# Attention of a two-block network: groups of heads in pairs, maxima ten steps ahead, weighing in halves of the queries

## The chip, the cores and the metric

The kernel runs on one core of a Trainium2 chip. The metric is the device time of one execution in microseconds; lower is better. The engines that matter here are TensorE (PE in the profile, with its weight loads as PEld), VectorE (DVE), ScalarE (ACT) and GpSimd (POOL). Each takes its own instructions strictly in order, and they wait for each other by semaphores.

## The reference

The network has two blocks over x of shape (8, 512, 128): attention with 16 heads and a mixture of experts, then a state-space layer and a second mixture of experts. Only the first attention is touched by the change:

```python
h = _layernorm(x, axis=-1) * (1 + ca) + sa
Q, K, V = (_lora_linear(h, W, b, A, B).reshape(8, 512, 16, 8) for q, k, v)
energy = jnp.einsum('nqhd,nkhd->nhqk', Q, K) / jnp.sqrt(8)
attn = jax.nn.softmax(energy, axis=-1)
out = jnp.einsum('nhqk,nkhd->nqhd', attn, V).reshape(8, 512, 128)
x = x + ga * _lora_linear(out, Wo, bo, Ao, Bo)
```

All of it is float32. The softmax subtracts each query's largest score, so the maxima have to be known before the exponentials.

## The kernel before

**Groups.** A head has 8 channels, so a 32-channel quarter of the 128 partitions holds four heads. A group g (32 of them: 8 batches by m = 0..3) is one head from each quarter, head 4j + m for j = 0..3. `split` (L465) writes the group's masked copies of queries and keys (`qt`, `kt`, 128x512) on POOL. The keys' copy carries a 1 in one otherwise unused row per quarter.

**Maxima.** For a unit u (a group's 128 queries, of which there are 4 x 32 = 128) `maxima` (L475) multiplies queries by keys into a pair of PSUM banks `pm` and DVE reduces each to its largest value, two heads at a time, into a padded tile `mpad`. When the four units of a group are through, `max_done` (L514) transposes `mpad` on PE (`pmt`, four transposes) and DVE subtracts the result from `qt`; the row of the queries' copy that meets the keys' 1 then holds minus the largest score.

**Scores, exponentials, weighing.** For a step t (a group's 128 keys) `scores` (L522) multiplies keys by queries into `ps`, one bank per head, and ACT takes the exponential into SBUF (`es`). `weigh` (L544) multiplies the values, 32 columns per head with a column of ones, by the exponentials: one call for 128 queries, 16 matmuls, into one bank `av`, which ACT copies to `part`. `normalise` (L564) transposes `part` back on PE (`ppt`), and DVE divides by the sums of the ones' column.

**Order.** The order is written out by hand. A step has two slots, so the 128 steps are slots 0 to 255; `slot` (L893) issues two score matmuls, two maxima matmuls of unit t + LEAD (LEAD = 6), two exponentials, one reduction, and then whatever `at_slot` has put into that slot. Units 0 to 5 come before slot 0, one in each second slot, through `maxima_first` (L495) with four matmuls and three reductions each, and small matmuls on the identity (`keep_busy`) between them. The last six steps have no maxima left. In the slots counted from a group's first one, a group's `split` is at -16, `max_done` at -3, `weigh` at 9, 11, 12 and 13, `normalise` at 15. A batch takes 32 slots, and what it needs besides (statistics of rows `load_stats` and `out_stats` on DVE, `load_batch`, `project_batch` with `pqk`, `values` with `pv`, `channels_back` with `pot` and `wo`, `out_proj` with `py`, and the routing of the tokens to experts) has slots of its own from L616 on; the slots of the routing are at L883 to L892.

**PSUM.** Of the eight banks four form the ring `sc` (`bank`, L307), which scores, `av`, `pmt`, `ppt` and all small results take in turn, each waiting until the tile four places before it has been read. The other four are two pairs `mx` (`pair`, L304) for the maxima and for `pqk`. All engine instructions but those of PE are issued by a helper, so the profile gives them line L65.

Of the kernel before, what the change touches and what calls it, by code (L numbers as in the profile page):

```python
# [10 lines left out]
FP = mybir.dt.float32  # L11
# [3 lines left out]
ALU = mybir.AluOpType  # L15
# [3 lines left out]
B, S, D = 8, 512, 128  # L19
P = 128  # L20
NC4 = S // P
NT = B * NC4
NE, NF = 8, 4
HD = 8
# [44 lines left out]
def tile_adaln_two_blocks(  # L69
# [41 lines left out]
    ident = ct([P, P], "ident")  # L111
# [62 lines left out]
    zeros = ct([P, P], "zeros")  # L174
    V.memset(zeros, 0.0)
    mpads = []
    for m in range(4):
        mp = ct([P, NC4, P], f"mpad{m}")
        G.memset(mp, 0.0)
        mpads.append(mp)  # L180
# [102 lines left out]

    mv1, rs1 = new_stats("l0a")
    mv2, rs2 = new_stats("l0f")
    LEAD = 6
    STEPS = 4 * 4 * B
    ES = 28
    kp = ctx.enter_context(tc.tile_pool(name="kp", bufs=1, side="right"))
# [2 lines left out]
    with tc.tile_pool(name="at", bufs=2) as at, tc.tile_pool(name="sc", bufs=4, space=PSUM) as psc, tc.tile_pool(  # L292
# [5 lines left out]
        for i in range(2):  # L298
            va = ate.tile([P, NC4, 16, 32], FP, tag=f"vaug{i}", name=f"vaug{i}")
            G.memset(va, 0.0)  # L300
            G.memset(va[:, :, :, HD], 1.0)
            vaugs.append(va)

        def pair(name):  # L304
# [146 lines left out]
        def values(b):  # L451
            ht = batch[b]["ht"]
            ps = bank("pv")
            for c in range(NC4):
                pin(
                    T.matmul(
                        ps[:, c, :], lhsT=ht[:, c * P : (c + 1) * P], rhs=wqk[:, 2, :], start=True, stop=True
                    )
                )
            A.copy(  # L460
                vaugs[b % 2].rearrange("p c h r -> p (c h) r")[:, :, 0:HD],
                flat(ps).rearrange("p (c d) -> p c d", d=HD),
            )

        def split(g):  # L465

            b, m = g // 4, g % 4
            sp = (m + 1) % 4
            qt = ate.tile([P, S], FP, tag="qt", name="qt", bufs=3)
            kt = ate.tile([P, S], FP, tag="kt", name="kt", bufs=3)  # L470
            (V if g == 0 else G).tensor_scalar(qt, batch[b]["q"], mask[:, m : m + 1], zero, ALU.mult, ALU.add)
            G.tensor_scalar(kt, batch[b]["k"], mask[:, m : m + 1], spare[:, sp : sp + 1], ALU.mult, ALU.add)
            group[g] = (qt, kt)

        def maxima(u, half):  # L475

            g, qc = u // 4, u % 4
            qt, kt = group[g]
            r0 = HD * ((g + 1) % 4)
            pm = pair("pm")  # L480
            for i in range(2):
                r = 32 * (2 * half + i)
                pin(
                    T.matmul(  # L484
                        pm[:, i, :],
                        lhsT=qt[r : r + 32, qc * P : (qc + 1) * P],
                        rhs=kt[r : r + 32, :],
                        start=True,
                        stop=True,
                    )  # L490
                )
            mp = mpads[g % 4][:, qc, :].rearrange("p (j r) -> p j r", r=32)
            return lambda: V.tensor_reduce(mp[:, 2 * half : 2 * half + 2, r0], pm, AX.X, ALU.max)

        def maxima_first(u):  # L495

            g, qc = u // 4, u % 4
            qt, kt = group[g]
            r0 = HD * ((g + 1) % 4)
# [9 lines left out]
            mp = mpads[g % 4][:, qc, :].rearrange("p (j r) -> p j r", r=32)  # L509
            V.tensor_reduce(mp[:, 0:2, r0], pm, AX.X, ALU.max)  # L510
            for j in (2, 3):
                V.tensor_reduce(mp[:, j : j + 1, r0], banks[j], AX.X, ALU.max)

        def max_done(g):  # L514

            qt, _ = group[g]
            pt = bank("pmt")
            for c in range(NC4):
                pin(T.transpose(pt[:, c, :], mpads[g % 4][:, c, :], ident))  # L519
            V.scalar_tensor_tensor(qt, flat(pt), -1.0, qt, ALU.mult, ALU.add)  # L520

        def scores(t, half):  # L522
            g, kc = t // 4, t % 4
# [17 lines left out]
                A.activation(es, ps, AF.Exp)  # L541
                es_of[t, j] = es

        def weigh(g, qc):  # L544

            b, m = g // 4, g % 4
            q = slice(P * qc, P * qc + P)
            ps = bank("av")
            for kc in range(NC4):
                for j in range(4):  # L550
                    pin(
                        T.matmul(  # L552
                            ps[32 * j : 32 * j + 32, 0, :],
                            lhsT=vaugs[b % 2][:, kc, 4 * j + m, :],
                            rhs=es_of[4 * g + kc, j][:, q],
                            start=(kc == 0),
                            stop=(kc == NC4 - 1),
                        )
                    )
            if qc == 0:  # L560
                part_of[g] = at.tile([P, NC4, P], FP, tag="part", name="part")
            A.copy(part_of[g][:, qc, :], ps[:, 0, :])

        def normalise(g):  # L564

            b, m = g // 4, g % 4
            part = part_of.pop(g)
            pt = bank("ppt")
            for c in range(NC4):
                pin(T.transpose(pt[:, c, :], part[:, c, :], ident))  # L570
            if m == 0:
                batch[b]["o"] = at.tile([P, NC4, D], FP, tag="o", name="o", bufs=1)
            p4 = pt.rearrange("p c (j r) -> p c j r", r=32)
            rd = stat.tile([P, NC4, 4], FP, tag="rd", name="rd")
            V.reciprocal(rd, p4[:, :, :, HD])
            o4 = batch[b]["o"].rearrange("p c (j m d) -> p c j m d", j=4, m=4)[:, :, :, m, :]
            V.tensor_tensor(o4, p4[:, :, :, 0:HD], rd.unsqueeze(3).to_broadcast([P, NC4, 4, HD]), ALU.mult)

        def channels_back(b):
            o = batch[b]["o"]  # L580
# [35 lines left out]
        at_slot(-42, silu_c)  # L616
        for t, n in ((-41, 9), (-31, 5), (-22, 3), (-16, 8), *((t, 5) for t in range(-11, 0, 2))):
            at_slot(t, lambda n=n: keep_busy(n))
        at_slot(-34, low_rank)
        at_slot(-33, lambda: modulation(0, mod0))  # L620
        at_slot(1, lambda: clamp(mod0, MOE_SCALE))
        at_slot(2, out_bias)
        at_slot(-9, lambda: modulation(1, mod1))
        at_slot(6, lambda: clamp(mod1, None))
        rows = ((gab, gab_rows), (mod0[:, 2, :], ga_rows), (mod0[:, 3, :], sb_rows), (mod0[:, 4, :], cb_rows))
        for i, (src, dst) in enumerate(rows):
# [1 line left out]
            at_slot(8 + i, lambda dst=dst, i=i: mod_rows_in(dst, i))  # L628
        for b in range(B):
            for c in range(NC4):  # L630
                at_slot(32 * b - 40 + c, lambda b=b, c=c: load_stats(b, c))
            if b == 0:
                at_slot(-35, lambda: load_root(0, 0))
                at_slot(-32, lambda: load_root(0, 1))
            else:
                at_slot(32 * b - 35, lambda b=b: load_root(b))
# [1159 lines left out]
```

## Time and profile before

| What | us |
|---|---|
| median of 3 runs | 1048.54 |
| lowest and highest run | 1046.57, 1048.92 |
| the profiled execution | 1048.89 |
| its span, first to last instruction | 1046.8 |
| first maxima matmul (L505) starts | 18.5 |
| first score matmul (L531) starts | 37.4 |
| last `av` matmul (L552) starts | 544.8 |

Attention therefore fills the stretch from 18.5 to about 546 us; the first mixture of experts follows, and its routing already runs on POOL and DVE within attention. The page gives each engine's busy time, the span in 40 slices, and the groups of like instructions. "idle before" is the time for which an engine stood still ahead of a group, and the arrow names what ended it.

### The profile page before, as it was taken

The numbers are of one execution on the slowest core, as the hardware profiler recorded it, in microseconds if no ns is written. First come the engines' busy times: TensorE is split into PE (matmuls) and PEld (weight loads), VectorE is DVE, ScalarE is ACT, GpSimd is POOL, SyncE is SP. The second block draws the span as 40 slices with busy tenths as digits, with TensorE's granted clock in tenths as the row PEclk, the third lists the DMA queues.
The fourth block names the chain that finished last, engine by engine and source line by source line (L and its number), as shares of the span: only waits on it lengthen the run. The fifth ranks groups of instructions, "written<-read, shape, count | busy, mean of one in ns | idle before, by whom it ended". The sixth has DMA issues, their size and how long they took to land.

```text
span 1046.8 us, 24415 instructions
## 1 busy us (share of the span) xinstructions
PE 1003.1 (96%) x9650; PEld 662.2 (63%) x9650; DVE 658.5 (63%) x1275; ACT 638.0 (61%) x1403; POOL 486.3 (46%) x764
## 2 busy tenths in 40 slices
PE   9999999999999999999999999999989978978888
PEld 7555555555555555555568989988778656655456
DVE  5968687777877777777712114136785649758572
ACT  1366667676766666666564655645686473685544
POOL 3313143463744547354364314278651457765651
PEclk9999999999999999999999999999999989999999
DMA  6099400000000000000126887722652043222051
GB/s 173 7 304 284 134 3 12 5 29 2 27 7 9 25 2 29 5 12 22 33 76 168 241 251 234 228 70 72 177 153 71 14 136 116 86 80 104 21 182 41
DMA packets 94771, 95.38 MB, mean 91 GB/s; under 512 B 7665, under 2 KB 72561, under 8 KB 94657
## 3 DMA queue, kind: packets, MB, share of 16 engines
q1 hardware_dynamic: 90384, 85.13, 26.7%
q0 software_dynamic: 4096, 8.40, 2.7%
q8 instruction: 76, 1.25, 0.5%
q14 instruction: 39, 0.31, 0.1%
q10 hardware_dynamic: 176, 0.30, 0.1%
HBM read 62.43 MB, written 31.36 MB: 90 GB/s over the span
## 4 chain that ended last, share of the span: by engine, by line
PE 76%; DVE 10%; POOL 5%; ACT 4%; issue 2%; DMA 2%; SPq 0%; ACTq 0%; POOLq 0%; DVEq 0%
PE ps L531 22%; PE av L552 11%; PE pyb L1044 9%; PE ph L1033 8%; PE pm L484 3%; DVE xc L65 2%; PE r L1440 2%; PE pe L1452 2%; PE pmt L519 2%; PE ppt L570 2%; PE pqk L444 1%; PE idle L417 1%; DVE sh L65 1%; PE pw L1352 1%; ACT L65 1%
## 5 line engine op out<-in xcount | busy, mean ns | idle before, releaser
L65 DVE TENSOR_REDUCE mpad<-pm 128x2 f32<-128x1024 f32 (+1 forms) x262 | 310.4, 1194 | 109.9 <-PE pm L484 106.8
L65 ACT ACTIVATE es<-ps 128x512 f32<-128x512 f32 x512 | 275.5, 598 | 161.3 <-PE pm L484 136.7
L531 PE MATMUL ps<-qt,kt 32*128 32x512 f32 x1024 | 291.2, 630 | 0.7 <-DVE x L65 0.6
L484 PE MATMUL pm<-kt,qt 32*128 32x512 f32 x976 | 261.5, 636 | 0.0
L552 PEld LDWEIGHTS av<-es,vaug 128*32 128x32 f32 x4096 | 104.2, 109 | 94.1 <-ACT part L65 43.2
L552 PE MATMUL av<-es,vaug 128*32 128x128 f32 x4096 | 137.7, 276 | 0.0
L531 PEld LDWEIGHTS ps<-qt,kt 32*128 32x128 f32 x1024 | 93.8, 183 | 61.2 <-issue 30.4
L65 ACT ACTIVATE hid<-ph,bias 128x256 f32<-128x256 f32 x184 | 72.0, 475 | 53.6 <-PE ph L1033 53.4
L786 POOL DMA_INDIRECT x_rows<-tok,ux x64 | 65.1, 1018 | 66.5 <-DMA x_rows<-tok,ux 58.4
L1044 PEld LDWEIGHTS pyb<-w2b,hid 128*128 128x128 f32 x736 | 89.7, 192 | 7.9 <-ACT hid L65 5.1
L1044 PE MATMUL pyb<-w2b,hid 128*128 128x128 f32 x736 | 91.2, 277 | 3.5 <-ACT hid L65 3.5
L1033 PE MATMUL ph<-xt,w1b 128*128 128x256 f32 x368 | 88.1, 383 | 0.0
L1064 POOL DMA_INDIRECT yg<-y_rows,yrows x64 | 66.8, 1043 | 35.9 <-issue 17.8
L484 PEld LDWEIGHTS pm<-kt,qt 32*128 32x128 f32 x976 | 73.2, 183 | 9.1 <-ACT kf L65 5.4
L65 POOL TENSOR_SCALAR qt<-qf,mask,zero 128x512 f32<-128x512 f32 x31 | 23.8, 768 | 110.1 <-PE pm L484 93.6
L1452 PE MATMUL pe<-x,l1w_sb 128*128 128x512 f32 x128 | 69.0, 635 | 4.6 <-ACT ye L65 4.5
L1033 PEld LDWEIGHTS ph<-xt,w1b 128*128 128x128 f32 x368 | 67.2, 193 | 7.5
L65 DVE COPY xt<-pxt 128x256 f32<-128x256 f32 x46 | 19.2, 419 | 76.2 <-PE pxt L958 76.2
L1440 PEld LDWEIGHTS r<-l1w_sb,t 128*128 128x128 f32 x368 | 47.9, 197 | 28.8 <-POOL t L65 13.7
L65 ACT ACTIVATE ye<-pe,pc 128x512 f32<-128x512 f32 x64 | 42.8, 682 | 37.3 <-PE pe L1452 28.3
L1440 PE MATMUL r<-l1w_sb,t 128*128 128x128 f32 x368 | 50.7, 283 | 10.8 <-POOL t L65 8.3
L65 DVE TENSOR_TENSOR t<-ye,gb 128x512 f32<-128x512 f32 x48 | 41.8, 892 | 1.8 <-DMA gb<-g_rows 0.9
(298 smaller groups left out, 1558.8 us busy)
## 6 DMA issues: line engine op xcount, KB each, us to landing
x_rows<-zeros SPq DMA_DIRECT2D x16, 1024.0 KB
gb<-g_rows SPq DMA_DIRECT2D x32, 512.0 KB
w1b<-in_w1t SPq DMA_DIRECT2D x46, 256.0 KB
w2b<-in_w2t SPq DMA_DIRECT2D x46, 256.0 KB
xg<-x_rows SPq DMA_DIRECT2D x46, 128.0 KB
y_rows<-yb SPq DMA_DIRECT2D x46, 128.0 KB
x<-in_x SPq DMA_DIRECT2D x8, 256.0 KB
h_chan<-hf SPq DMA_DIRECT2D x8, 256.0 KB
```

The lines of the kernel that those rows point to most:

```text
L65: return lambda *args, **kwargs: self.pin(call(*args, **kwargs))
L484: T.matmul(pm[:, i, :], lhsT=qt[r : r + 32, qc * P : (qc + 1) * P], rhs=kt[r : r + 32, :], start=True, stop=True,)
L519: pin(T.transpose(pt[:, c, :], mpads[g % 4][:, c, :], ident))
L531: T.matmul(ps, lhsT=kt[r : r + 32, kc * P : (kc + 1) * P], rhs=qt[r : r + 32, :], start=True, stop=True)
L552: T.matmul(ps[32 * j : 32 * j + 32, 0, :], lhsT=vaugs[b % 2][:, kc, 4 * j + m, :], rhs=es_of[4 * g + kc, j][:, q], start=(kc == 0), stop=( ...
L570: pin(T.transpose(pt[:, c, :], part[:, c, :], ident))
L786: nc.gpsimd.indirect_dma_start(out=x_rows[h], out_offset=IndirectOffsetOnAxis(ap=chosen["ux", b][:, k, c : c + 1], axis=0), in_=half[h]["t ...
L1033: pin(T.matmul(ph[:, f, :], lhsT=it["w1"][:, f * P : (f + 1) * P], rhs=it["x"], start=True, stop=True))
L1044: T.matmul(py[:, c, :], lhsT=it["hid"][:, f, c * P : (c + 1) * P], rhs=it["w2"][:, f, :], start=(f == 0 and "shared" not in it), stop=(f = ...
L1064: nc.gpsimd.indirect_dma_start(out=gathered[b][:, k, c, :], out_offset=None, in_=y_rows[h], in_offset=IndirectOffsetOnAxis(ap=half[h]["yro ...
L1440: T.matmul(ffn[b]["r"][:, c, :], lhsT=x[:, c * P : (c + 1) * P], rhs=w, start=(start and c == 0), stop=stop, skip_group_check=True,)
L1452: pin(T.matmul(pe, lhsT=l1w_sb[:, 2 + e, :], rhs=x1s[b], start=True, stop=True))
```

## The change

Two groups of one batch, g even and g + 1, become a pair.

- **Maxima in pairs.** The maxima of both groups go into one `mpad` tile, each in its own unused row of a quarter, so `max_done` runs once for a pair (slot -3 of its even group): four transposes, then two subtractions on DVE, one for each `qt`. Two `mpad` tiles are left of four.
- **LEAD is 10 instead of 6,** since both groups' maxima must be through before the even group's scores start. `split` moves from slot -16 to -24, and `qt` and `kt` get four buffers instead of three. Ten units come before slot 0.
- **Values.** The 32 columns of a head hold the 8 values and the column of ones at 0 to 8 for even m and at 16 to 24 for odd m. ACT's copy of a batch's values becomes two copies of half the size.
- **Weighing in halves.** One call handles 256 queries: 16 matmuls of 256 columns, in slots 9 and 12. The even group's result is copied to `part` by ACT; the odd group's is added to `part` by DVE.
- **Normalising in pairs.** One `normalise` per pair, at slot 23 of the even group: four transposes, one reciprocal and one product of twice the size.
- **Everything that feeds a batch** (`load_stats`, `load_root`, `load_batch` but for its middle step, `project_batch`) moves 8 slots ahead, `values` from slot 2 to slot -4 of its batch; the preparation before slot 0 moves 8 slots ahead too. The routing stays in its slots.

```diff
-    LEAD = 6
+    LEAD = 10
@@
-            A.copy(
-                vaugs[b % 2].rearrange("p c h r -> p (c h) r")[:, :, 0:HD],
-                flat(ps).rearrange("p (c d) -> p c d", d=HD),
-            )
+            for e in range(2):
+                A.copy(
+                    vaugs[b % 2].rearrange("p c (n e) r -> p (c n) e r", e=2)[:, :, e, 16 * e : 16 * e + HD],
+                    flat(ps).rearrange("p (n e d) -> p n e d", e=2, d=HD)[:, :, e, :],
+                )
@@
         def max_done(g):
-            qt, _ = group[g]
             pt = bank("pmt")
             for c in range(NC4):
-                pin(T.transpose(pt[:, c, :], mpads[g % 4][:, c, :], ident))
-            V.scalar_tensor_tensor(qt, flat(pt), -1.0, qt, ALU.mult, ALU.add)
+                pin(T.transpose(pt[:, c, :], mpads[g // 2 % 2][:, c, :], ident))
+            for k in range(2):
+                qt, _ = group[g + k]
+                V.scalar_tensor_tensor(qt, flat(pt), -1.0, qt, ALU.mult, ALU.add)
@@
-        def weigh(g, qc):
+        def weigh(g, h):
...
-            q = slice(P * qc, P * qc + P)
-            ps = bank("av")
+            q = slice(2 * P * h, 2 * P * h + 2 * P)
+            ps = flat(bank("av"))[:, 0 : 2 * P]
...
-            if qc == 0:
+            if g % 2:
+                part = flat(part_of[g - 1])[:, q]
+                V.tensor_tensor(part, part, ps, ALU.add)
+                return
+            if h == 0:
                 part_of[g] = at.tile([P, NC4, P], FP, tag="part", name="part")
-            A.copy(part_of[g][:, qc, :], ps[:, 0, :])
+            A.copy(flat(part_of[g])[:, q], ps)
@@
         for g in range(4 * B):
-            at_slot(8 * g - 16, lambda g=g: split(g))
-            at_slot(8 * g - 3, lambda g=g: max_done(g))
-            for qc in range(NC4):
-                at_slot(8 * g + (9, 11, 12, 13)[qc], lambda g=g, qc=qc: weigh(g, qc))
-            at_slot(8 * g + 15, lambda g=g: normalise(g))
+            at_slot(8 * g - 24, lambda g=g: split(g))
+            if g % 2 == 0:
+                at_slot(8 * g - 3, lambda g=g: max_done(g))
+                at_slot(8 * g + 23, lambda g=g: normalise(g))
+            for h in range(2):
+                at_slot(8 * g + (9, 12)[h], lambda g=g, h=h: weigh(g, h))
@@
-                at_slot(32 * b - 40 + c, lambda b=b, c=c: load_stats(b, c))
+                at_slot(32 * b - 48 + c, lambda b=b, c=c: load_stats(b, c))
...
-            for i, s in enumerate((-30, 20, -24)):
+            for i, s in enumerate((-38, 20, -32)):
...
-                at_slot(32 * b - 18 + i, lambda b=b, i=i: project_batch(b, i))
-            at_slot(32 * b + 2, lambda b=b: values(b))
+                at_slot(32 * b - 26 + i, lambda b=b, i=i: project_batch(b, i))
+            at_slot(32 * b - 4, lambda b=b: values(b))
```

More of the change, by code (lines that the diff above doesn't have):

```diff
@@ L176, in tile_adaln_two_blocks @@
     mpads = []
-    for m in range(4):
+    for m in range(2):
         mp = ct([P, NC4, P], f"mpad{m}")
@@ L300, in tile_adaln_two_blocks @@
             G.memset(va, 0.0)
-            G.memset(va[:, :, :, HD], 1.0)
+            for e in range(2):
+                G.memset(va.rearrange("p c (n e) r -> p c n e r", e=2)[:, :, :, e, 16 * e + HD], 1.0)
             vaugs.append(va)
@@ L459, in values @@
                 )
-            A.copy(
-                vaugs[b % 2].rearrange("p c h r -> p (c h) r")[:, :, 0:HD],
-                flat(ps).rearrange("p (c d) -> p c d", d=HD),
-            )
+            for e in range(2):
+                A.copy(
+                    vaugs[b % 2].rearrange("p c (n e) r -> p (c n) e r", e=2)[:, :, e, 16 * e : 16 * e + HD],
+                    flat(ps).rearrange("p (n e d) -> p n e d", e=2, d=HD)[:, :, e, :],
+                )
         def split(g):
             b, m = g // 4, g % 4
-            sp = (m + 1) % 4
-            qt = ate.tile([P, S], FP, tag="qt", name="qt", bufs=3)
-            kt = ate.tile([P, S], FP, tag="kt", name="kt", bufs=3)
+            sp = (m + 2) % 4
+            qt = ate.tile([P, S], FP, tag="qt", name="qt", bufs=4)
+            kt = ate.tile([P, S], FP, tag="kt", name="kt", bufs=4)
             (V if g == 0 else G).tensor_scalar(qt, batch[b]["q"], mask[:, m : m + 1], zero, ALU.mult, ALU.add)
@@ L478, in maxima @@
             qt, kt = group[g]
-            r0 = HD * ((g + 1) % 4)
+            r0 = HD * ((g + 2) % 4)
             pm = pair("pm")
@@ L491, in maxima @@
                 )
-            mp = mpads[g % 4][:, qc, :].rearrange("p (j r) -> p j r", r=32)
+            mp = mpads[g // 2 % 2][:, qc, :].rearrange("p (j r) -> p j r", r=32)
             return lambda: V.tensor_reduce(mp[:, 2 * half : 2 * half + 2, r0], pm, AX.X, ALU.max)
@@ L498, in maxima_first @@
             qt, kt = group[g]
-            r0 = HD * ((g + 1) % 4)
+            r0 = HD * ((g + 2) % 4)
             pm = pair("pm")
@@ L508, in maxima_first @@
                 )
-            mp = mpads[g % 4][:, qc, :].rearrange("p (j r) -> p j r", r=32)
+            mp = mpads[g // 2 % 2][:, qc, :].rearrange("p (j r) -> p j r", r=32)
             V.tensor_reduce(mp[:, 0:2, r0], pm, AX.X, ALU.max)
@@ L552, in weigh @@
                         T.matmul(
-                            ps[32 * j : 32 * j + 32, 0, :],
+                            ps[32 * j : 32 * j + 32, :],
                             lhsT=vaugs[b % 2][:, kc, 4 * j + m, :],
@@ L572, in normalise @@
                 batch[b]["o"] = at.tile([P, NC4, D], FP, tag="o", name="o", bufs=1)
-            p4 = pt.rearrange("p c (j r) -> p c j r", r=32)
-            rd = stat.tile([P, NC4, 4], FP, tag="rd", name="rd")
+            p4 = pt.rearrange("p c (j e r) -> p (c j) e r", j=4, e=2)
+            rd = stat.tile([P, NC4 * 4, 2], FP, tag="rd", name="rd")
             V.reciprocal(rd, p4[:, :, :, HD])
-            o4 = batch[b]["o"].rearrange("p c (j m d) -> p c j m d", j=4, m=4)[:, :, :, m, :]
-            V.tensor_tensor(o4, p4[:, :, :, 0:HD], rd.unsqueeze(3).to_broadcast([P, NC4, 4, HD]), ALU.mult)
+            o4 = batch[b]["o"].rearrange("p c (j m d) -> p (c j) m d", j=4, m=4)[:, :, m : m + 2, :]
+            V.tensor_tensor(o4, p4[:, :, :, 0:HD], rd.unsqueeze(3).to_broadcast([P, NC4 * 4, 2, HD]), ALU.mult)
         def channels_back(b):
@@ L609, in tile_adaln_two_blocks @@
         for g in range(4 * B):
-            at_slot(8 * g - 16, lambda g=g: split(g))
-            at_slot(8 * g - 3, lambda g=g: max_done(g))
-            for qc in range(NC4):
-                at_slot(8 * g + (9, 11, 12, 13)[qc], lambda g=g, qc=qc: weigh(g, qc))
-            at_slot(8 * g + 15, lambda g=g: normalise(g))
-        at_slot(-42, silu_c)
-        for t, n in ((-41, 9), (-31, 5), (-22, 3), (-16, 8), *((t, 5) for t in range(-11, 0, 2))):
+            at_slot(8 * g - 24, lambda g=g: split(g))
[4 more added lines that the diff above has]
+                at_slot(8 * g + (9, 12)[h], lambda g=g, h=h: weigh(g, h))
+        at_slot(-50, silu_c)
+        for t, n in ((-49, 9), (-39, 5), (-30, 3), (-24, 8), *((t, 5) for t in range(-19, 0, 2))):
             at_slot(t, lambda n=n: keep_busy(n))
-        at_slot(-34, low_rank)
-        at_slot(-33, lambda: modulation(0, mod0))
+        at_slot(-42, low_rank)
+        at_slot(-41, lambda: modulation(0, mod0))
         at_slot(1, lambda: clamp(mod0, MOE_SCALE))
         at_slot(2, out_bias)
-        at_slot(-9, lambda: modulation(1, mod1))
+        at_slot(-13, lambda: modulation(1, mod1))
         at_slot(6, lambda: clamp(mod1, None))
@@ L630, in tile_adaln_two_blocks @@
             for c in range(NC4):
-                at_slot(32 * b - 40 + c, lambda b=b, c=c: load_stats(b, c))
+                at_slot(32 * b - 48 + c, lambda b=b, c=c: load_stats(b, c))
             if b == 0:
-                at_slot(-35, lambda: load_root(0, 0))
-                at_slot(-32, lambda: load_root(0, 1))
-            else:
-                at_slot(32 * b - 35, lambda b=b: load_root(b))
-            for i, s in enumerate((-30, 20, -24)):
+                at_slot(-43, lambda: load_root(0, 0))
+                at_slot(-40, lambda: load_root(0, 1))
+            else:
+                at_slot(32 * b - 43, lambda b=b: load_root(b))
+            for i, s in enumerate((-38, 20, -32)):
                 at_slot(32 * b + s, lambda b=b, i=i: load_batch(b, i))
             for i in range(2):
-                at_slot(32 * b - 18 + i, lambda b=b, i=i: project_batch(b, i))
-            at_slot(32 * b + 2, lambda b=b: values(b))
+                at_slot(32 * b - 26 + i, lambda b=b, i=i: project_batch(b, i))
+            at_slot(32 * b - 4, lambda b=b: values(b))
             at_slot(32 * b + 42, lambda b=b: channels_back(b))
```

## The prediction

> **What bounds the kernel now.** I read the page's busy shares first, then the groups by shape, then the timeline of one stretch of eight slots, and last the waits at attention's end.
>
> ```profile
> PE 1003.1 (96%) x9650; PEld 662.2 (63%) x9650; DVE 658.5 (63%) x1275; ACT 638.0 (61%) x1403; POOL 486.3 (46%) x764
> ...
> L65 DVE TENSOR_REDUCE mpad<-pm 128x2 f32<-128x1024 f32 (+1 forms) x262 | 310.4, 1194 | 109.9 <-PE pm L484 106.8
> L65 ACT ACTIVATE es<-ps 128x512 f32<-128x512 f32 x512 | 275.5, 598 | 161.3 <-PE pm L484 136.7
> L531 PE MATMUL ps<-qt,kt 32*128 32x512 f32 x1024 | 291.2, 630 | 0.7 <-DVE x L65 0.6
> ```
>
> PE looks full, and DVE and ACT seem to wait for it. That is half of it: a matmul that waits inside a stretch still shows as busy. The timeline of the slots between two `av` blocks shows the other half. Columns: start, length, engine, instruction; in brackets the idle time before it.
>
> ```profile
> 93.41 0.70 PE L531 MATMUL ps<-qt,kt 32*128 32x512 f32 x2
> ...
> 93.59 0.69 DVE L65 SCALAR_TENSOR_TENSOR qt<-pmt,qt 128x512 f32<-128x512 f32 x1 [0.36 <-PE pmt L519]
> ...
> 94.67 2.36 DVE L65 TENSOR_REDUCE mpad<-pm 128x2 f32<-128x1024 f32 x2 [0.39 <-PE pm L484]
> ...
> 96.94 0.25 DVE L65 RECIPROCAL rd<-ppt 128x16 f32<-128x16 f32 x1
> ...
> 97.23 0.29 DVE L65 TENSOR_TENSOR o<-ppt,rd 128x128 f32<-128x128 f32 x1
> 97.44 1.22 DVE L65 TENSOR_REDUCE mpad<-pm 128x2 f32<-128x1024 f32 x1
> ...
> 97.67 0.19 PEld L484 LDWEIGHTS pm<-kt,qt 32*128 32x128 f32 x2
> ...
> 98.73 0.54 PE L552 MATMUL av<-es,vaug 128*32 128x128 f32 x12
> ```
>
> Slots 6, 7, 0 and 1 of a group run here (counted from a group's first; 93.41 to 98.73, 5.32 us) with one `ppt` among them. DVE is idle for nothing from 94.67 on: two reductions, reciprocal, product, reduction. The last slot's matmuls start at 97.67, when the product has freed `ppt`'s bank in the ring of four. So **between `av` blocks DVE sets the pace**, and in an `av` block PE does, while DVE rests.
>
> **The rates.** From this timeline: a slot's first reduction starts 1.26 us after the slot, each further one 1.14 us later; a slot issued right behind another costs PE 0.86, behind an `av` or a transpose 0.97; from the last slot's matmuls to the next `av` it is 1.06. The chain of waits has each `av` block at 1.01 us. A slot n may put its maxima into PSUM only when reduction n - 2 is done (two pairs), and the maxima stand behind the scores in PE's queue. Slots 1 to 5 with their four `av` and `pmt` take 8.7 us, so a group without a batch's extra work takes 14.0 (8 slots); the measured batch of 32 slots takes 63.8 (slots 128 to 159), 7.8 of it extras.
>
> **Part 1: fewer PE instructions.** An `av` block's 32 records go in 8 rounds of four; rounds start 0.109 us apart, and 0.14 is entry and exit. Twice the columns: the score matmuls with 512 columns have rounds of 0.43, so 256 take 0.216, and a block 8 x 0.216 + 0.14 = **1.86 us** instead of 2 x 1.01; the bounds are 1.0 (width free) and 2.0. PE's bare sum for a pair of groups, with a block counted 0.09 longer behind a slot that starts early, is before 16 x 0.86 + 8 x 1.10 + 10 x 0.12 (slots behind another kind of work) + 4 x 0.6 (`pmt`, `ppt`) = 26.2, and after 16 x 0.86 + 4 x 1.95 + 6 x 0.12 + 2 x 0.6 = 23.5.
>
> Here two rules pull apart. The Trainium skill's page Perfetto Trace Analysis (Identifying Performance Opportunities) says that larger matmuls are more efficient where possible; by it the 16 pairs would give 16 x 2.7 = 43 us. TensorEngine Tiling (Array Packing), under Performance Considerations, PSUM Bottleneck, says that tiling speeds up TensorE but not the emptying of PSUM, which can become the limit. The row above (1.14 us per slot on DVE, untouched by the change) says which one holds here, so I sum by stretches.
>
> **Part 2: the stretches between the wider blocks.** `av` now falls into slots 1, 4, 9, 12 of 16. No trace shows these; each is built from the rates above.
> - Slots 2 to 4, and 10 to 12 (three each): the third waits for the first reduction, 1.26 + 1.23 + 1.06 = 3.5.
> - Slots 5 to 9, with `ppt` after slot 7: reductions 5, 6, 7, then reciprocal and product of twice the size (0.25 and 0.29 become about 0.27 and 0.42) free the bank that slot 9 needs: 1.26 + 3 x 1.14 + 0.8 + 1.06 = 6.6.
> - Slots 13 to 1, with `pmt` after slot 13: reduction 13, two subtractions (0.69 each, 0.65 in a row), which free the bank of slot 15's second score; its maxima, reduction 15, slot 1: 3.8 to the bank, 1.2 to the maxima, 1.25, 1.06 = 7.35.
> - The sum with four blocks is 3.5 + 6.6 + 3.5 + 7.35 + 4 x 1.86 = **28.4 for two groups, against 28.0 before.** The saving of PE is gone: DVE had a rest at four `av`, now at two longer ones per group.
> The odd group's addition (128x256, between the 0.29 us product and the 0.69 us subtraction, so 0.42) waits for its block's end, but the next reduction comes 1.26 later; it costs nothing there. ACT's copy grows to 0.376 (the `yb` copy of that size), the two of a batch's values to 0.75 from 0.58, both beside DVE.
>
> **Part 3: a batch's extras.** In the slots where DVE sets the pace PE work hides: `ptf` costs nothing (0.9 before), `pot` 0.5 (0.9), `pv` 0.8 (1.3), `pqk` 2.5 (3.7 with `py` and `pcount`). `ptn` and `pl` at slot 0 cost 1.1. DVE work now hurts more: `py`'s addition (0.68) at slot 14 and both sets of statistics (0.46 a row) at slots 15 to 19, with the two subtractions close by, cost 1.5. Together 6.4, so a batch is 4 x 14.2 + 6.4 = 63.2. As each sum lets a stretch begin with empty queues, I add 0.4: 63.6 against 63.8. Over the seven batches' worth of full slots **-1.7 us**, -0.8 for the first two groups (no `pv`, `pmt` in slots 2 and 5).
> On POOL `load_root` (2.4 us) and `load_batch` (four of 0.79) move in front of the tokens' product that `ptf` waits for. In before it ends at 280.4 and `ptf` starts at 284.3; the scatters there wait about 1.5 us for each other's landing and hide most of the move, so `ptf` keeps 2.4 us of air. Without that air, +1 to 3 us per batch.
>
> **Part 4: LEAD.** Before slot 0, DVE is the bound:
>
> ```profile
> 18.40:37.40 19.00, 18.91 (x126) 12.20 (x126) 16.20 (x30) 0.47 (x1) 5.77 (x12) 1.00 0.01 1
> ...
> 519.70:552.00 32.30, 29.39 (x419) 18.29 (x416) 7.46 (x22) 20.88 (x48) 20.74 (x40) 1.00 0.29 86
> ```
>
> (By stretch: length, then busy time of PE, PEld, DVE, ACT, POOL.) A unit costs three reductions, 1.14 + 0.6 + 0.6 = 2.34; four more and a second subtraction are 4 x 2.34 + 0.65 = **+10.0 us**. The same maxima leave the end: slots 236 to 243 have none and become 17.5 -> about 13 in length, and the last statistics of batch 6 come some **-5.5** earlier. The last slots give nothing more: from 521 POOL has a closed chain (root, four scatters 2.5 us apart, the tokens' product, four tables of 1.9) that ends in `wo` at 551.3, and PE stands for it (`py` waits for POOL's `wo`, 4.2 us). Were POOL not late, 4 us more.
>
> **Sum.** +10.0 - 0.8 - 1.7 - 5.5 = +2.0 on the profiled 1048.89, which lies 0.35 over the median of the runs: 1050.9, rounded to **1051**.
>
> **Rivals.**
> - *PE was the bound after all, and its saving arrives.* If DVE's pace costs only half of what I reckon (the reductions are 1.14 in a row, and DVE waits 109.9 us for PE in all), half of 43 arrives: -21.5 + 10 - 5.5 = -17: 1032; a third, -14, gives 1039. Against it: the stretch above.
> - *Slower, by DVE's fullest stretch.* Slots 13 to 19 once a batch hold seven reductions, two subtractions, one `py` addition, eight rows of statistics. If a subtraction or the statistics there hold back one slot more than I count (0.75 us in each of a batch's two such stretches, two thirds of a reduction), or POOL's tokens are late for `ptf`, a batch costs 1.5 more: 2.0 + 7 x 1.5 = +12: 1061. It decides as soon as a batch of 32 slots exceeds the present 63.8, since nothing then pays for LEAD.
> - *No change:* the hand sums without my 0.4 give -0.8 us, 1048.
>
> **Chances.** The measurement tells apart about 0.2%, 2.1 us. My case, a small loss of 0 to 5 us, 0.35; the slow rival 0.27; no change or a small gain 0.2; PE's saving 0.18. That gives slower 0.50, same 0.17, faster 0.33. The likeliest case alone spans 1048 to 1055; the range to hold eight of ten is 1039 to 1063.
>
> **What would show it.** First score matmul at 47.4 +- 1; `av` blocks of 1.86; a batch of 63 to 64 us; slots 13 to 1 (with `pmt`) 7.3 and slots 5 to 9 6.6 from slot to `av`, the wait ended by DVE; POOL's chain before `wo` as long as now. A batch under 62 would prove me wrong toward faster, over 64.5 toward slower.

## The result and the profile after

| | before | after |
|---|---|---|
| median, us | 1048.73 (1046.57 to 1049.05, 4 runs) | 1057.69 (1056.13 to 1059.2, 4 runs) |
| span of the profiled execution | 1046.8 | 1054.3 |

The ratio is **1.0098, with an interval of 1.0077 to 1.0118**: slower, by more than forecast. The four runs of the kernel after lie in two pairs, 1056.1 to 1056.4 and 1059.0 to 1059.2, and the profiled one (1056.13) is of the lower pair, so the two profiles differ by 7.5 where the medians differ by 9.0; no run here explains the pairs. The page's busy shares and groups of the kernel after:

```profile
PE 1006.2 (95%) x7514; PEld 637.7 (60%) x7514; DVE 660.2 (63%) x1279; ACT 614.7 (58%) x1315; POOL 484.9 (46%) x764
...
L65 DVE TENSOR_REDUCE mpad<-pm 128x2 f32<-128x1024 f32 (+1 forms) x266 | 308.3, 1179 | 110.4 <-PE pm L488 104.4
L65 ACT ACTIVATE es<-ps 128x512 f32<-128x512 f32 x512 | 269.5, 604 | 131.3 <-PE pm L488 99.1
L537 PE MATMUL ps<-qt,kt 32*128 32x512 f32 x1024 | 297.6, 625 | 0.6 <-DVE x L65 0.5
```

PE has 2136 matmuls fewer (9650 before) and is busy for 3.1 us more. The reductions stand where they stood (308.3 against 310.4 us of work, 110.4 against 109.9 of idle time before them). Matmuls went away on PE; none of that became time. Where the two executions differ is seen by marking when a slot's first score matmul starts (S n for slot n):

| stretch | before, us | after, us | difference | forecast |
|---|---|---|---|---|
| start to S0 | 37.4 | 48.2 | +10.8 | +10.0 |
| S0 to S16 | 30.2 | 31.2 | +1.0 | -0.8 |
| S16 to S236 | 434.7 | 434.9 | +0.2 | -1.7 |
| S236 to S244 | 17.5 | 13.8 | -3.7 | -5.5 |
| S244 to the last `py` | 32.1 | 32.0 | -0.1 | 0 |
| a batch (mean of slots 64 to 191) | 63.83 | 63.84 | +0.01 | -0.2 |

The five stretches give +8.2, which is how much later the last `py` starts (551.84 and 560.09); the first tile of the experts (`pxt`, 546.43 and 553.95) and the end come 7.5 later. So **the ten units of maxima ahead of slot 0, four more than before, are the loss, and the batches, which were to pay for them, take just as long as before.**

Stretches by length and busy time (of PE, PEld, DVE, ACT, POOL; then the granted clock) of the kernel after, the one before slot 0 and the four middle batches:

```profile
18.50:48.20 29.70, 29.34 (x204) 19.15 (x204) 25.79 (x42) 1.93 (x3) 9.73 (x17) 1.00 0.00 1
172.54:427.91 255.37, 253.20 (x2291) 123.64 (x2288) 191.41 (x277) 161.28 (x329) 130.62 (x250) 1.00 0.04 13
```

and the same four batches of the kernel before:

```profile
158.97:414.31 255.34, 255.22 (x3378) 137.73 (x3377) 190.68 (x277) 173.33 (x374) 130.69 (x251) 1.00 0.04 14
```

A third fewer matmuls, the same DVE work, a full clock in both, the same length to 0.03 us in 255. Neither DVE (75% of the stretch) nor ACT (63%) is full. The timeline around one of the wider `av` blocks of the kernel after (start, length, engine, instruction, idle time before it) shows why they still matter:

```profile
239.96 1.93 PE L558 MATMUL av<-es,vaug 128*32 128x256 f32 x32
240.05 1.08 ACT L65 ACTIVATE es<-ps 128x512 f32<-128x512 f32 x2 [0.79 <-PE pm L488]
240.15 1.23 DVE L65 TENSOR_REDUCE mpad<-pm 128x2 f32<-128x1024 f32 x1 [1.19 <-PE pm L488]
...
242.03 0.42 DVE L65 TENSOR_TENSOR part<-part,av 128x256 f32<-128x256 f32 x1 [0.66 <-PE av L558]
...
242.98 3.05 ACT L65 ACTIVATE es<-ps 128x512 f32<-128x512 f32 x6 [1.85 <-PE pm L488]
243.09 1.23 DVE L65 TENSOR_REDUCE mpad<-pm 128x2 f32<-128x1024 f32 x1 [0.63 <-PE pm L488]
...
243.63 0.29 PEld L537 LDWEIGHTS ps<-qt,kt 32*128 32x128 f32 x2 [0.64 <-ACT es L65]
```

During the 1.93 us of the block ACT and DVE finish one slot's work (1.08 and 1.23 us) and run dry: ACT for 1.85 us, DVE for 0.66 and 0.63 around its addition. Then ACT takes six exponentials in 3.05, 1.02 us for the two of a slot, and a reduction in a row costs 1.14: near each other, and both longer than the 0.86 that PE needs for a slot. The block starves both, and afterwards the next scores' weight loads wait for ACT (0.64 us in the last line). Between 100 and 500 us (engine, tile and line, what it waited for: total us, times, longest), first of the kernel before, then of the kernel after:

```profile
PEld ps L531 <- ACT es L65: 8.9, 39, 0.4
```

```profile
PEld ps L537 <- ACT es L65: 34.2, 91, 0.6
```

The weight loads of the scores wait for the exponentials nearly four times as long as before.

### The profile page after: what moved, and what is told of

The parts are those of the page before. It is cut to its first block, busy times and chain, and to the rows that moved or that the text cites. A ratio compares the mean times of both kernels' runs of the same rounds, so it can differ in the third digit from the quotient of the medians.

```text
span 1054.3 us, 20042 instructions
## 1 busy us (share of the span) xinstructions
PE 1006.2 (95%) x7514; PEld 637.7 (60%) x7514; DVE 660.2 (63%) x1279; ACT 614.7 (58%) x1315; POOL 484.9 (46%) x764
## 4 chain that ended last, share of the span: by engine, by line
PE 78%; DVE 10%; POOL 6%; ACT 3%; issue 2%; DMA 1%; SPq 0%; POOLq 0%; DVEq 0%; ACTq 0%
PE ps L537 21%; PE av L558 10%; PE pyb L1055 9%; PE ph L1044 8%; PE pm L488 6%; DVE xc L65 2%; PE r L1451 2%; PE pe L1463 2%; PE idle L419 2%; PE pqk L446 1%; PE pm L509 1%; DVE mpad L65 1%; DVE sh L65 1%; PE pw L1363 1%; PE pyb L1014 1%
## 5 line engine op out<-in xcount | busy, mean ns | idle before, releaser
L65 DVE TENSOR_REDUCE mpad<-pm 128x2 f32<-128x1024 f32 (+1 forms) x266 | 308.3, 1179 | 110.4 <-PE pm L488 104.4
L65 ACT ACTIVATE es<-ps 128x512 f32<-128x512 f32 x512 | 269.5, 604 | 131.3 <-PE pm L488 99.1
L537 PE MATMUL ps<-qt,kt 32*128 32x512 f32 x1024 | 297.6, 625 | 0.6 <-DVE x L65 0.5
L488 PE MATMUL pm<-kt,qt 32*128 32x512 f32 x944 | 250.3, 630 | 0.9 <-ACT kf L65 0.9
L537 PEld LDWEIGHTS ps<-qt,kt 32*128 32x128 f32 x1024 | 111.1, 183 | 106.9 <-issue 50.1
L558 PE MATMUL av<-es,vaug 128*32 128x256 f32 x2048 | 123.6, 382 | 0.0
L558 PEld LDWEIGHTS av<-es,vaug 128*32 128x32 f32 x2048 | 60.1, 109 | 80.2 <-ACT es L65 31.1
```

Source lines behind the costliest of these rows:

```text
L65: return lambda *args, **kwargs: self.pin(call(*args, **kwargs))
L488: T.matmul(pm[:, i, :], lhsT=qt[r : r + 32, qc * P : (qc + 1) * P], rhs=kt[r : r + 32, :], start=True, stop=True,)
L537: T.matmul(ps, lhsT=kt[r : r + 32, kc * P : (kc + 1) * P], rhs=qt[r : r + 32, :], start=True, stop=True)
L558: T.matmul(ps[32 * j : 32 * j + 32, :], lhsT=vaugs[b % 2][:, kc, 4 * j + m, :], rhs=es_of[4 * g + kc, j][:, q], start=(kc == 0), stop=(kc ...
```

## The experiments

The theory on record was: between `av` blocks the reductions on DVE set the pace. The rivals were that PE's instructions themselves are the bound, and, formed after the first four runs, a **second theory: two rings, each two slots deep, hold the slots apart together** (the pairs `pm`, emptied by the reductions, and the ring `sc`, emptied by the exponentials), and either one alone nearly keeps the pace.

The runs fall in three groups, each on another chip (12, 11 and 3 in the record): the kernel before had a median of 1048.27 us in the first (lead, halves, both kernels with shorter maxima), 1074.47 in the second (shorter exponentials, both cuts, slots 8 and 10 without pairs) and 1074.15 in the third (the rest). In the last two the added time lies behind attention: the run with slots 8 and 10 reaches the experts' first tile at 539.6, where the kernel before took until 546.4 in its profile, and needs 529.1 us from there to its span's end instead of 500.4. (All eight profiles of these two groups show a granted clock of 0.5 for 24 to 27 us somewhere between 664 and 726 us, and none of the first group does; with slots 8 and 10 PE is busy for only 25.7 us of the 40 from 680 on. What stops it there is not known.) Hence ratios to the kernel before of the same group are compared, and the length of a batch (same clock of 1.00; the kernel with slots 8 and 10 has 63.09 on two of the chips); over eight batches 1 us is worth 8, or 0.8%.

| kernel | ratio to before (interval) | batch, us |
|---|---|---|
| after | 1.0098 (1.0077 to 1.0118) | 63.84 |
| before, LEAD alone | 1.0065 (1.0041 to 1.0089) | 64.08 |
| before, halves alone | 1.0077 (1.006 to 1.0094) | 65.21 |
| after, maxima over half the keys | 0.9848 (0.9832 to 0.9865) | 61.13 |
| before, maxima over half the keys | 0.9917 (0.9901 to 0.9934) | 63.32 |
| after, half the exponentials | 0.9987 (0.9969 to 1.0005) | 62.81 |
| after, both cuts | 0.9667 (0.9623 to 0.971) | 58.94 |
| before, both cuts | 0.9822 (0.9782 to 0.9862) | 62.25 |
| after, `max_done` behind `av` | 1.0057 (1.0034 to 1.008) | 63.45 |
| before, `av` in slots 8, 10, 12, 13 | 0.9916 (0.9891 to 0.9941) | 63.09 |
| pairs with quarters | 0.994 (0.9911 to 0.9969) | 62.20 |
| before, slots 8, 10, early `wo` | 0.9911 (0.9881 to 0.9941) | 63.09 |
| pairs with quarters, slots 8, 10, early `wo` | 0.9906 (0.9872 to 0.994) | 61.95 to 62.3, mean 62.12 |

### LEAD alone

```diff
-    LEAD = 6
+    LEAD = 10
@@
-            at_slot(8 * g - 16, lambda g=g: split(g))
+            at_slot(8 * g - 24, lambda g=g: split(g))
```

(with the batches' feeding steps 8 slots earlier and four `qt` and `kt`, as in the change; to make room two `tok` instead of three and one `wo`)

> The kernel before with LEAD 10 and all that must move with it (split, loads, projection and values 8 slots earlier, four buffers of qt and kt), but no pairs and weighing in quarters; to make room, tok has two buffers and wo one. Theory (the start is DVE's, four units more cost 4 x 2.34, and only about 5 us come back at the end): first score matmul at 47 us instead of 37.4, a batch of 32 slots still near 63.8, in all +4 to +7, so 1053 to 1056. Rival (a longer lead costs nothing, the loss sits in the pairs and halves): within 2 us of 1048.7.

Measured: +7.8 us (1056.07 against 1048.27), a little more than the 4 to 7 expected. S0 comes at 48.2, as in the whole change, S236 to S244 takes 14.2, and the batch 64.08. LEAD alone costs nearly what the whole change costs; pairs and halves together take 0.24 us off its batch. What the fewer `tok` and `wo` buffers add was not tried apart.

### Halves alone

```diff
-            q = slice(P * qc, P * qc + P)
+            q = slice(2 * P * h, 2 * P * h + 2 * P)
@@
-                at_slot(8 * g + (9, 11, 12, 13)[qc], lambda g=g, qc=qc: weigh(g, qc))
+                at_slot(8 * g + (9, 12)[h], lambda g=g, h=h: weigh(g, h))
```

> The kernel before with one part of the change alone: weighing in halves of the queries in slots 9 and 12, every result copied by ACT; LEAD 6, no pairs. Theory (DVE sets the pace between av blocks and loses two of its four rests): av blocks of 1.86 us, a plain group about 14.3 instead of 14.0, the batch 64 to 66, total 1050 to 1064. Rival (PE sets the pace): the batch loses 8 x 0.16 and half of the layout changes, at least 1.3 us, in all -9 or better, 1040 or below.

Measured: +8.5 us (1056.77 against 1048.27), the batch +1.38. The four middle batches of the kernel with halves alone, to be held against the line of the kernel before:

```profile
162.97:423.79 260.82, 260.82 (x2353) 124.66 (x2352) 188.49 (x277) 169.02 (x342) 131.15 (x251) 1.00 0.04 13
```

A thousand matmuls fewer, a little less work on DVE and on ACT, and 5.5 us more in time: halves are a loss at LEAD 6 and without pairs too, and with every result copied by ACT, so the change's addition on DVE is not the reason. A plain group (slots 22 to 29 of a batch) takes 15.0 us instead of 14.0; the theory's sum had asked for 14.3. The part changes two things at once, the width of a block and the distance between blocks.

### Shorter maxima, in both kernels

```diff
-            return lambda: V.tensor_reduce(mp[:, 2 * half : 2 * half + 2, r0], pm, AX.X, ALU.max)
+            return lambda: V.tensor_reduce(mp[:, 2 * half : 2 * half + 2, r0], pm[:, :, 0 : S // 2], AX.X, ALU.max)
```

In the kernel after:

> The changed kernel with the maxima in the slots reduced over the first 256 keys only (left out: the other half of the keys in the maximum; PE still computes all). A reduction takes about 0.65 instead of 1.22 us. Theory (DVE's pace between av blocks is the bound in both kernels): the batch falls from 63.8 to PE's own sum, 53 to 57, total about 1000 to 1015. Rival (a chain of POOL, or ACT and the ring of banks, gives both kernels the same 63.8): the batch stays above 62, total above 1045.

In the kernel before:

> The kernel before with the same shortened reductions in the slots (left out: half of the keys in the maximum). Theory: the batch falls less, from 63.8 to 57 to 60, since PE's bare sum is 2.7 us per pair of groups larger than in the changed kernel; total 1008 to 1025, so that with DVE out of the way the changed kernel is the faster one by about 5 to 20 us, LEAD's cost included. Rival (another bound common to both): the batch stays above 62, total above 1038, and the order of the two does not turn.

Measured: batches of 61.13 (-2.7) and 63.32 (-0.5). Both missed what the first theory asked for (53 to 57 and 57 to 60), by 4.1 and 3.3 us. With DVE busy for 127 us of the four batches' 245 the kernel after should have run free. Waits of DVE between 100 and 500 us (engine, tile and line, what it waited for: total us, times, longest), first of the kernel after, then with its maxima shortened:

```profile
DVE mpad L65 <- PE pm L488: 91.5, 95, 2.9
```

```profile
DVE mpad L65 <- PE pm L488: 152.2, 131, 3.4
```

DVE's freed time has become waiting. It is fed no faster, so **the first theory falls as stated**. What stays of it: the two kernels change places (1032.85 against 1039.87), so DVE is part of what hides PE's saving.

### Shorter exponentials, and both cuts

```diff
-                A.activation(es, ps, AF.Exp)
+                A.activation(es[:, 0 : 2 * P], ps[:, 0 : 2 * P], AF.Exp)
@@
-                            rhs=es_of[4 * g + kc, j][:, q],
+                            rhs=es_of[4 * g + kc, j][:, 0 : 2 * P],
```

In the kernel after:

> The changed kernel with exponentials of the first 256 queries only, which weigh reads for both halves (left out: the other half of the exponentials); reductions whole, PE's work unchanged. Second theory (two rings hold the slots apart, each two slots deep: the pairs emptied by DVE's reductions and the ring of four emptied by ACT's exponentials, and either alone nearly keeps the pace): the batch falls as little as with the short reductions, from 63.8 to 60.5 to 63, total 1030 to 1053. First theory (DVE alone sets the pace): within 0.4 of 63.8. Rival (ACT is the bound by itself): below 58, total below 1020.

Together with the shorter maxima:

> The changed kernel with both cuts, half of the maxima's keys and half of the exponentials (both left out as named). Second theory: only now does PE's own sum show, the batch falls by much more than the two single cuts together (about 3 each), to 53 to 57, total 985 to 1012. First theory: as with the short reductions alone, 61. A bound elsewhere (POOL, the program's order): not below 59.

The same pair of cuts in the kernel before (there each quarter of the weighing reads the first or the second 128 of the 256 exponentials):

> The kernel before with the same two cuts. Second theory: PE's bare sum is larger here, so the batch goes to 57 to 60, 2 to 4 us above the changed kernel with both cuts; total 1005 to 1025. If the saving of PE by pairs and halves is not real, both kernels come to the same batch within 1 us.

Measured in the kernel after: -1.0 by the exponentials alone, -2.7 by the maxima alone, and **-4.9 by both, more than the 3.7 of their sum**: each cut alone is held back by the engine that was left whole. But the 53 to 57 that the second theory asked for with both cuts is missed by 2 us: 58.94 stands at the edge of the third case named beforehand, a bound elsewhere that keeps the batch from falling below 59. So it is shown that DVE and ACT hold the pace together; that it comes of rings two slots deep is argued, for no run changed their depth (all eight banks are in use). In the kernel before both cuts bring only -1.6. The four batches of the kernel after with both cuts:

```profile
158.53:394.27 235.74, 232.89 (x2294) 115.59 (x2290) 126.89 (x276) 112.56 (x328) 129.72 (x249) 1.00 0.04 14
```

and of the kernel before with both:

```profile
150.10:399.09 248.99, 248.99 (x3377) 132.89 (x3377) 124.56 (x277) 123.17 (x373) 130.44 (x251) 1.00 0.04 14
```

With the same light load on DVE and ACT the change makes four batches 13.3 us shorter, 3.3 per batch. That is PE's saving; it exists, though smaller than the 2 x 2.7 of the bare sums. And the kernel before, with a third of its DVE work and nearly a third of its ACT work taken out, still takes 62.25 of its 63.83, where 57 to 60 was expected. What holds it there is not shown: that PE is busy throughout (248.99 of 248.99) does not decide it, since it is so in the kernel with halves alone too (260.82 of 260.82), at a longer time.

### `max_done` behind the `av` block

```diff
-                at_slot(8 * g - 3, lambda g=g: max_done(g))
+                at_slot(8 * g - 4, lambda g=g: max_done(g))
```

> The changed kernel with max_done one slot earlier, in slot -4 of the pair, right behind the av block of slot 12, so that the two subtractions run while DVE rests. Second theory (the stretch of slots 13 to 1 is held by the subtractions that keep the bank of pmt and delay the reductions): its 7.9 and 8.4 us in a batch fall by 0.5 to 0.9 each, the batch goes from 63.84 to 62.0 to 62.9, and the time to 0.998 to 1.004 of the kernel before (the changed kernel itself: 1.0098). Rival (the subtractions are covered): batch within 0.3 of 63.84, ratio 1.008 to 1.012.

Measured: 63.45, -0.39, where 0.9 to 1.8 less was expected. In slots 12 to 17 nothing is won (12.8 us, now 13.1); the gain lies at the batch's end (slots 28 to 31: 9.6, now 9.0). Where `max_done` stands is a small part of what is lost.

### Blocks spread out without pairs

```diff
-                at_slot(8 * g + (9, 11, 12, 13)[qc], lambda g=g, qc=qc: weigh(g, qc))
+                at_slot(8 * g + (8, 10, 12, 13)[qc], lambda g=g, qc=qc: weigh(g, qc))
```

> The kernel before with the four weighings of a group in slots 8, 10, 12 and 13 instead of 9, 11, 12 and 13 (same work, only the longest stretch without av shortened from four slots to three). Second theory: slots 14, 15 and 0 with ppt then take about 3.5 instead of 5.3 for four, the stretch costs PE's own time, a plain group goes from 14.0 to 13.1 to 13.5 and the batch to 60 to 62.5; total 1022 to 1040, faster than both kernels. Rival (PE's order and its sum hold the 14.0): within 4 us of 1048.

Measured: 63.09 (-0.74), less than expected, but faster beyond doubt (0.9916). The gain is not where it was expected: a plain group (slots 22 to 29), for which 13.1 to 13.5 was named, takes 14.1 as against 14.0. It lies in slots 30 to 13, across the batch's end, which go from 31.9 to 30.9 us. So to cut the plain group's longest stretch without `av` from four slots to three won nothing there; what makes the gain is not known.

### Pairs, but weighing in quarters

The change with its pairs, its LEAD and its moved values, and the kernel before's four blocks in slots 9, 11, 12, 13; the even group's are copied by ACT, the odd group's added by DVE in four pieces.

```diff
-            for h in range(2):
-                at_slot(8 * g + (9, 12)[h], lambda g=g, h=h: weigh(g, h))
+            for qc in range(NC4):
+                at_slot(8 * g + (9, 11, 12, 13)[qc], lambda g=g, qc=qc: weigh(g, qc))
```

> The changed kernel with weighing in quarters again (slots 9, 11, 12, 13; even groups copied by ACT, odd ones added by DVE): pairs and LEAD 10 without halves. Second theory: LEAD alone was +7.8 and the halves alone +8.0, so the pairs must be worth about -8: the batch 62.0 to 62.8, first scores still at 48, ratio to the kernel before 0.997 to 1.003. Rival (the halves are good inside pairs, their loss belongs to the old order): batch 63.8 or more, ratio above 1.006.

Measured: 62.20 as expected, and a ratio of 0.994, a little better than expected: **faster than before**. (S0 comes at 46.0 instead of the 48 expected; the last section has the reason.) It has a thousand matmuls more than the change in these batches and is 1.64 us per batch shorter:

```profile
167.51:416.31 248.80, 248.80 (x3316) 133.08 (x3313) 193.04 (x292) 164.68 (x344) 130.06 (x250) 1.00 0.04 14
```

Its timeline at the block in the same place of the order as the wider block shown above:

```profile
233.22 1.08 PE L558 MATMUL av<-es,vaug 128*32 128x128 f32 x32
233.31 1.09 ACT L65 ACTIVATE es<-ps 128x512 f32<-128x512 f32 x2 [0.70 <-PE pm L488]
233.41 1.23 DVE L65 TENSOR_REDUCE mpad<-pm 128x2 f32<-128x1024 f32 x1 [1.10 <-PE pm L488]
...
234.56 0.28 DVE L65 TENSOR_TENSOR part<-part,av 128x128 f32<-128x128 f32 x1
...
235.39 2.07 ACT L65 ACTIVATE es<-ps 128x512 f32<-128x512 f32 x4 [1.00 <-PE pm L488]
235.50 1.23 DVE L65 TENSOR_REDUCE mpad<-pm 128x2 f32<-128x1024 f32 x1 [0.66 <-PE pm L488]
```

A block of 1.08 us is as long as the two exponentials that lie beside it (1.09). Behind it ACT stands still for 1.00 us instead of 1.85 and DVE for 0.66 instead of 0.66 and 0.63: in the change the block outlasts the exponentials by 0.85. Over the four batches (length less busy time) DVE is idle for 55.8 us instead of 64.0, and ACT for 84.1 instead of 94.1.

### Early `wo`, with and without pairs

The last `py` of the kernel after waits for POOL (timeline; the bracket is the idle time of PE):

```profile
560.09 1.70 PE L605 MATMUL py<-wo,ot 128*128 128x128 f32 x8 [1.90 <-POOL wo L65]
```

`wo` does not depend on the batch's attention, so it can be made in a batch's slot 20 (the two lines that make it in `channels_back` are taken out):

```diff
+                wo = batch[b]["wo"] = at.tile([P, D], FP, tag="wo", name="wo")
+                G.tensor_tensor(wo, wqk[:, 3, :], ga_rows[:, b, :], ALU.mult)
```

On top of the kernel with slots 8 and 10:

> The kernel before with the weighings in slots 8, 10, 12, 13 (as in the run before, 0.9916) and the product wo issued on POOL in slot 20 of its batch instead of slot 42, ahead of the tables and the ranking. If PE stands for POOL's wo at attention's end, as the prediction has it, the last py comes 2 to 4 us earlier and the ratio is 0.986 to 0.990; if another link of POOL's chain is as late, 0.990 to 0.993.

On top of pairs with quarters, with slots 8, 10, 12, 13 as well:

> Pairs and LEAD 10 with quarters in slots 8, 10, 12, 13 and the early wo: the parts together that should be worth something. Batch 61.2 to 62.3, first scores at 48, ratio 0.986 to 0.996. If it is not below the spread kernel with early wo, pairs do not pay for their LEAD.

Measured: without pairs, the last `py` no longer waits for POOL and comes 3.0 us earlier (S244 to `py` shrinks from 33.6 to 30.4), but the experts' first tile starts only 0.9 us earlier (538.7 instead of 539.6), and the ratio (0.9911, not 0.986 to 0.990) cannot be told from 0.9916. With pairs the batch is about 1 us shorter and that tile starts at 535.2, but the ratio is 0.9906. Both kernels beat the kernel before by about 0.9%; the runs do not tell them apart, so by the mark set beforehand pairs are not shown to pay for their LEAD once the blocks are spread.

## Why the prediction was right or wrong

- **Direction and ground: right; size: too small.** PE's saving doesn't arrive, LEAD isn't paid for. The measured median lies in the range, but 6.7 us above the forecast of 1051 and outside the likeliest case (1048 to 1055). The slow rival came nearer in size, yet not by its way: it wanted a batch of 65, and the batch is 63.84.
- **"Between `av` blocks DVE sets the pace": the step that failed.** DVE's cut alone frees 2.7 us of a batch and ACT's 1.0, both 4.9. I showed ACT's line with its 161.3 us of idle time and went on with DVE alone, without asking what a second ring two slots deep does when its 1.02 to 1.08 us per slot are so near DVE's 1.14. The waits that I wanted "ended by DVE" are, where the scores' weight loads show them, ended by ACT (34.2 us). The stretches I built from DVE's rates came out near all the same, most of the forecasts a little short: slots 2 to 4 in 3.69 (forecast 3.5), 5 to 9 with `pqk` in 9.24 (6.6 + 2.5), 10 to 12 with `pot` in 3.94 (3.5 + 0.5), 13 to 17 in 7.92 (7.35 and a part of the 1.5 for `py` and the statistics), 18 to 20 in 3.93 (3.5), a plain 5 to 9 in 7.06 (6.6), 13 to 1 across the batch's end in 8.38 (7.35 + 1.1). That is luck in part: ACT's pace is almost DVE's, and the 0.4 added per batch made up for part of the rest. A sum that fits was no proof of its mechanism; only the cuts told.
- **"The saving of PE is gone": right, and now in parts.** 63.83 of the batch before, +0.25 by LEAD (64.08), -1.88 by the pairs (62.20 with quarters), +1.64 by the halves, make 63.84; added in another order the parts differ (halves alone +1.38). I had put the wider blocks' loss down to DVE's "two longer" rests; ACT rests longer still (1.85 us), and PE pays for both.
- **The two rules.** The sentence of the Trainium skill on larger matmuls stands in Perfetto Trace Analysis under Optimizing Tensor Performance (Matmuls), not under the section that I named. With DVE and ACT relieved the change is worth 3.3 us per batch, about 26 in all instead of the 43 reckoned by it; with both at full work, nothing. Here the emptying of PSUM decides, as I said, but by two engines and not by DVE's 1.14 us alone.
- **The block: right.** The next slot starts 1.86 us after it, as forecast from rounds of 0.216 (1.93 from its first start to its last end).
- **Part 4, LEAD: +10.8 for +10.0.** DVE's busy time before slot 0 grows by 9.6 (16.20 to 25.79); I left out that its idle time grows too, from 2.8 to 3.9.
- **The first two groups: +1.0 for -0.8.** LEAD alone gives the same 31.2 for S0 to S16, so LEAD is enough for it; halves alone give 30.7 and pairs with quarters 31.9, so it is no plain sum of the parts. Which of LEAD's steps does it wasn't tried.
- **The batches: +0.2 for -1.7.** A batch is 63.84 where the sum said 63.6; over seven, that is the difference.
- **The end: -3.7 for -5.5.** Slots 236 to 243 take 13.8, not 13, and the slots behind them keep their 19 us. POOL's chain is as I put it, only later: `wo` starts at 559.6 instead of 551.3. PE's wait for it I had at 4.2 us; that is the sum of the matmul's 1.9 and the weight load's 2.3, which run at the same time, so 1.9 is what a punctual POOL could save.

These four terms miss by 0.8, 1.8, 1.9 and 1.8, all to the same side: 6.3 us up to the last `py`, of which 5.5 are left at the end of the profiled span; the rest of the median's 6.7 is not in these two profiles. A likely reason, not shown: my stretches each began with empty queues, and the few tenths that this leaves out were added once, as 0.4 per batch; the start and the end got none.

What stays open: with both cuts the kernel after needs 58.94 per batch and the kernel before 62.25, while PE's bare sums by the prediction's rates are some 54 and 59 (twice 23.5 and twice 26.2, and about 6.5 of extras). The third slot of a stretch (slots 4, 20, 28) still takes 1.34 to 1.41 us up to its `av` in the kernel after with both cuts, where slots 9 and 12 take 0.95. That the time from a score matmul to its exponential (1.16 us) is to blame would be a guess; it wasn't tried.

## What to carry to other kernels

When PE feeds two engines through rings that hold two slots of work, count in slots of their work, not in PE instructions: a block on PE that lasted longer than one slot of theirs (here 1.93 against 1.08 and 1.23 us) left both engines idle, and the matmuls it saved came back as waits. So try such blocks at the length of the work beside them. No run here changed the width and kept the distance between blocks, so how much each of the two does is open. An engine that is 60% busy is not ruled out as a bound; halve its work alone, then the other's, then both, and see whether the gains add up. And take a change's parts one at a time: here pairs with their LEAD took 1.6 us off a batch, and the halves that came with them put the same 1.6 back.

## What was not expected of the hardware

- The small matmuls that keep PE busy at the start came 0.213 us apart until about 13.5 us and 0.11 us apart from then on in the kernel before, and the profile grants the full clock from 13.5: the clock's rise can be read from the spacing of a row of equal matmuls. Kernels with the same instructions before slot 0 differ in it (the change, and the change with shorter maxima). In seven of the fourteen profiles the full clock that lasts comes at 13.5 to 16.1 us and the first maxima at 18.3 to 18.7; in the other seven at 11.2 to 12.4 and at 15.8 to 16.4, in each of the three groups. So S0 of two runs is to be compared only with the first maxima beside it: the 48.2 of the change and of LEAD alone go with 18.5, the 46.0 of pairs with quarters with 16.4.
- At attention's end PE stands still for 1.9 us until `wo` is there, and about 1 us later the granted clock falls to 0.5 for 3.4 us, at 552.8 in the kernel before and at 560.5 in the kernel after. The wait alone does not bring it: the run with slots 8 and 10 has the same 1.9 us and keeps the clock of 1.00 there.
